# Linear attention gated by a Hadamard FFN on one core: spare VectorE work only where it fits, down's weights worked on 16 places behind their loads, layernorms queued in the output projection

## The chip, the cores and the metric

The kernel runs on one core of a Trainium2 chip. The metric is the device time in microseconds, as the median of several runs. The engines are named as in the profile: PE is TensorE (PEld its weight loads), DVE is VectorE, ACT is ScalarE, POOL is GpSimd, and SP is SyncE, which here does nothing but start DMA transfers, one after the other.

## The reference

`x` has 8 sequences of 512 tokens and 512 columns, all in float32. What is computed:

```python
xn  = layernorm(x)                                   # over the 512 columns
q, k, v = (xn @ W.T + b for W, b in ((Wq, bq), (Wk, bk), (Wv, bv)))
kv  = cumsum((elu(k) + 1) * v, axis=tokens)          # elementwise, along the sequence
s   = ((elu(q) + 1) * kv * 32**-0.5) @ Wo.T + bo
h   = fwht(xn * SU_ug) / 64                          # Walsh-Hadamard transform over 512 columns
up, gate = h @ W_up.T * scale_up, h @ W_gate.T * scale_gate      # 512 -> 2048
h   = fwht(silu(gate) * up * SU_dp) / 64             # over 2048 columns
g   = silu(h @ W_down.T * scale_dp)                  # 2048 -> 512
out = x + s * g
```

## The kernel before

**Tiling.** Two sequences make a pair, and the main loop runs over four pairs, p = 0 to 3. Every large product is a fast product: both operands are combined into seven factors (P1 to P7, each a sum or difference of quarters), seven half-size products are made, and VectorE adds them together while it reads them from PSUM. The weights' factors are made once, at p = 0, by VectorE and GpSimd, stored to DRAM (`keep_w`, `inner_w` with `d_gu`, `down_w` with `d_down`), and loaded from there in every later pair (`stream_w`). For `down`, whose weights also take the Hadamard transform, p = 0 first runs a chain over four blocks of 128 columns: load a block (`load_down`, L1062), scale it and run four butterfly levels on VectorE (`butterflies_down`, L1073 and L1078), let PE apply the remaining 128-point transform (`fold_down`, the four `pwd` matmuls of L1092), scale on ScalarE, store to `wd_f` (L1101). Then `first_half_down` loads it back by rows, encodes the factors and stores them in `d_down_0`, from which `w_down` is loaded.

**A pair.** `attention` makes k, v and q with cumsum and context; then four units u = 0 to 3 of the FFN follow: `gate` and `up` at p = 0, `hidden_unit` at p = 1 to 3 (it transforms with Hadamard levels on VectorE and GpSimd, whose result is `ho`). The output projection `project_out` (matmul L645, names `px_o`, `py_o`, `pz_o`) is interleaved with the end of unit 0. `down` runs after units 1 and 3. In between, tokens of the next pair are prepared: `normalized(b)` loads a sequence, takes its statistics (L201, L202), the root (L205), scales it (L210, L211) and stores it as `d_x`; `times_scales` multiplies by SU_ug on GpSimd and stores `d_xs`; `transforms` runs the Hadamard levels; `next_tokens` loads `z_x` and transposes it into the factors `xa`.

**Order.** The tile framework orders the instructions of each engine by priority, and each engine then executes its own list strictly in order; a wait at the head of it holds all that follows. Three devices set the order here:

- an agenda: `at(place, fn)` has a step issued `place` places later, where a place is two matmul instructions of 128x512 (0.86 us of PE) and `advance(n)` moves on;
- two lists of spare VectorE work: `later(us, fn, soon=)` queues a step with the time it is thought to take, in `urgent` (soon) or `idle`; `pace(ins, us)` issues from them behind a PSUM read `ins`, for about `us`; `catch_up()` issues all that is left at the end of a stage;
- `background()`, which lowers the priority by 150.

A weight is asked for by `ask(3)`, three entries ahead in a queue; `get_w` puts its encoding steps on the agenda. Buffers: six tiles in the pool `t8`, one in `xin`, four weights in `wpool`, PSUM banks px 3, py 1, pz 2, t 2.

The matmul lines are L569 (q, k, v, gate, up), L645 (o, down) and L747 (gate and up in `hidden_unit`). The PSUM reads of VectorE are L585 (at L569), L656 and L660 (at L645), L757 to L789 (at L747). ScalarE makes the snapshots `sa`, `sb`, `sc` of partial sums at p = 0 (L579, L581).

Two lines matter for what follows. In `inner_w` the fourth combination is written in the slot of the first, whose store must have landed:

```python
later(1.0, made, P5, 0, w1[:, 0], w1[:, 1], ALU.add, soon=True)
...
later(1.0, made, P7, 0, w0[:, 0], w1[:, 0], ALU.subtract, soon=True)
```

Of the kernel before, what the change touches and what calls it, by code (L numbers as in the profile page):

```python
# [21 lines left out]
def kernel(  # L22
# [67 lines left out]
    def pace(ins, us):  # L90
        while us > 0 and (urgent or idle):
            t, fn, args = (urgent or idle).pop(0)
            with tc.issue_after(ins.ins):
                fn(*args)
            us -= t
# [83 lines left out]
    def normalized(b, delay=12):  # L179


        if b > 3:
            t = xin.tile([P, 3, 7, P], F32, tag="x", name=f"x_{b}").rearrange("p c s e -> p (c s e)")
            xt = t[:, : NT * D].rearrange("p (n d) -> p n d", n=NT)
            su = t[:, NT * D : (NT + 1) * D]
        else:
            xt = t8.tile([P, NT, D], F32, tag="t", name=f"x_{b}")
        load_x(b, xt)
        if b > 3:
            nc.sync.dma_start(su, su_row.rearrange("o d -> (o d)").partition_broadcast(P))  # L190
        mv = small.tile([P, NT, 2], F32, tag="mv", name=f"mv_{b}")
# [28 lines left out]
        def times_scales():  # L220
            for t in range(NT):
                nc.gpsimd.tensor_tensor(xt[:, t], xt[:, t], su, ALU.mult)
            put("xs")
            if b % 2 == 0:
                at(8, lambda: normalized(b + 1, 10))

        def start():
            if b > 3:
                with background():
                    for t in range(NT):  # L230
                        stats(t)
                    root()
                    for t in range(NT):
                        scaled(t)
                    store()
                return
            for t in range(NT):
                later(0.8, stats, t)
            later(0.3, root)
            for t in range(NT):  # L240
                later(0.6, scaled, t)
            later(0.0, store)
# [45 lines left out]
    def next_tokens(b, xa):  # L288

        za, z = squares(f"x_{b}", xin), squares(f"x_{b + 1}", t8)  # L290
        turned(xa, P1, za, 0)
        turned(xa, P2, za, 1)

        def rest():
            turned(xa, P7, z, 0)
            turned(xa, P3, z, 1)
            outer_factors(xa)

        at(10, rest)

# [139 lines left out]
    def stream_w(name):  # L440
        w = new_w("%s_%s" % (name[0], name[1] if type(name[1]) is int else "%d_%d" % name[1]))
        if name[0] == "gu":
            u, i = name[1]
            nc.sync.dma_start(w, inner[u][:, i])
        elif name[0] == "down":
            h, i = name[1]
            while wd_made[h] < 4:
                assert urgent or idle
                _, fn, args = (urgent or idle).pop(0)
                fn(*args)  # L450
            w = by_factor(w, 4)
            nc.sync.dma_start(w, wd[h][:, i])
        else:
            nc.sync.dma_start(flat(w), kept["%s_%d" % name])
            if name[0] == "o":
                w = by_factor(w)
# [53 lines left out]
    def inner_w(m, u, w0, w1):  # L510
# [19 lines left out]
        later(1.0, made, P3, 2, w0[:, 1], t[:, 1], ALU.subtract, soon=True)  # L530
        later(1.0, made, P7, 0, w0[:, 0], w1[:, 0], ALU.subtract, soon=True)

# [268 lines left out]
    def attention(p, xo, co, get_w):  # L801
        def project(m, g, then):
# [4 lines left out]
            def whole(px):  # L807
# [4 lines left out]
                f"{m}_{p}_{g}", [w[:, 0], w[:, 1]], x_rhs(xo),  # L812
                (r[:, 0, 0], r[:, 1, 0], r[:, 1, 1]), whole, b, 1.7,
            )

        def elu_plus_one(r, name, then=None):
# [9 lines left out]
            half(0)  # L826
            at(5, lambda: half(1))

# [215 lines left out]
    def hidden_w(name, src, f):  # L1044
# [9 lines left out]

        return w, [(11, encode)]

# [5 lines left out]
    def load_down(o):  # L1062
        loaded.append(o)
        nc.sync.dma_start(rs[:, o % 2], wdown_t[:, o * P : (o + 1) * P].rearrange("(c p) e -> p c e", p=P))
# [48 lines left out]
    def first_w(m, g):  # L1113
# [4 lines left out]
        if m == "up":  # L1118
            return hidden_w(m, wup_t, g)
        name, eng = f"{m}_{g}", nc.gpsimd if m == "o" else nc.vector  # L1120
        if m == "o":
# [31 lines left out]
    def ask(n):  # L1153
        while queue and len(ahead) < n:
            p, m, g = queue.pop(0)
            w, steps = (first_w if p == 0 and m != "down" else later_w)(m, g)
# [68 lines left out]
    def begin_down():  # L1225
        nc.sync.dma_start(wsc_r, wscale_dp.partition_broadcast(P))
        load_down(0)
        at(12, lambda: chain_down(0))

    def chain_down(o):  # L1230
        if o not in loaded:
            at(4, lambda: chain_down(o))
            return

        def folded_block():
            fold_down(o)
            if o + 2 < KD:
                at(8, lambda: load_down(o + 2))
            if o + 1 == KD:
                at(8, first_half_down)  # L1240

        def then():
            at(14, folded_block)
            if o + 1 < KD:
# [5 lines left out]
        13: [lambda: normalized(2)], 14: [lambda: normalized(3)],  # L1250
        0: [lambda: first_transform(0, xa, xp, hads)], 1: [lambda: first_transform(1, xa, xp, hads)], 2: [begin_down],
        3: [lambda: load_down(1)], 4: [lambda: nc.sync.dma_start(bo_r, bo.partition_broadcast(P))],
    }
# [24 lines left out]
    for p in range(B // 2):  # L1278
# [12 lines left out]
        for u in range(NU):  # L1291
# [8 lines left out]
            else:  # L1300
                ho = new_h(f"ho_{p}_{u}")
                hidden_unit(p, u, xp, ho, get_w, u % 2 == 1)
                if u == 0 and more:
                    normalized(2 * p + 2)
                if u == 0:
# [67 lines left out]
```

## Time and profile before

| | |
|---|---|
| median of 3 runs | 1605.88 us (1604.14 to 1606.89) |
| the profiled execution | 1604.9 us |
| its span | 1603.1 us |
| granted TensorE clock, mean | 0.988 |
| PE busy | 1531.3 us (96%) |
| DVE, ACT, POOL busy | 1069.6, 394.8, 461.7 us |
| bytes moved by DMA | 285.74 MB, 178 GB/s over the span |

A row of the timeline has the start and the duration in microseconds from the start of the span, the engine, the line of the kernel, the operation, the tiles written and read by their names, the shape and the count; in brackets is how long the engine had been idle before, and what it was waiting for. A matmul in float32 counts twice in the profile, so four of 128x512 are two instructions of the kernel. A row of the groups has the busy time and the mean of one in nanoseconds, then the idle time before such rows with what ended most of it.

### The profile page before, as it was taken

The page shows a single profiled execution, that of the slowest core. Times are in us where ns is not written, and L with a number is a line of the kernel's source. Part 1 is how long each engine was busy: PE and PEld are TensorE (multiplying, and loading weights), DVE is VectorE, ACT ScalarE, POOL GpSimd, SP SyncE. Part 2 cuts the span into 40 slices and gives each one's busy share as a digit, 9 for nine tenths or more (in the row PEclk, how much of TensorE's full clock was granted, in tenths as well). Part 3 has the DMA queues.
Part 4 walks back from the last instruction along what each step waited for, and adds up shares of the span by engine and source line. Part 5 has one row for each costly group of instructions (what it writes and reads, how often), then busy time and mean ns, then how long its engine had stood idle before and what let it go on. Part 6 is the DMA issues. An engine that isn't in the chain of part 4 may idle for free. (4 is left out here: it accounts for less than half of the span.)

```text
span 1603.1 us, 15445 instructions
## 1 busy us (share of the span) xinstructions
PE 1531.3 (96%) x5808; PEld 1102.9 (69%) x5808; DVE 1069.6 (67%) x1444; ACT 394.8 (25%) x611; POOL 461.7 (29%) x262
## 2 busy tenths in 40 slices
PE   6987999999899999999999997999999999999998
PEld 3433636744674588788884486888887458888887
DVE  6896774465448984878664886688674686552673
ACT  4343321122014521112113431111211441111211
POOL 1034044012420363304510155300632116120731
PEclk9998999999999999999999999999999999999999
DMA  8327688776963357365677354736486524425462
GB/s 251 98 86 198 185 266 275 228 214 200 278 183 120 120 194 225 126 211 168 186 238 173 112 168 161 239 112 242 143 259 174 136 87 138 170 89 183 146 253 95
DMA packets 249034, 285.74 MB, mean 178 GB/s; under 512 B 98944, under 2 KB 200832, under 8 KB 244864
## 3 DMA queue, kind: packets, MB, share of 16 engines
q1 hardware_dynamic: 248288, 284.72, 57.7%
q8 instruction: 46, 0.75, 0.2%
q14 instruction: 28, 0.23, 0.0%
q10 hardware_dynamic: 672, 0.03, 0.0%
HBM read 200.31 MB, written 84.41 MB: 178 GB/s over the span
## 5 line engine op out<-in xcount | busy, mean ns | idle before, releaser
L645 PE MATMUL px_dn<-w_down,ho 128*128 128x256 f32 x1024 | 228.5, 379 | 0.0
L645 PEld LDWEIGHTS px_dn<-w_down,ho 128*128 128x128 f32 x1024 | 194.6, 190 | 28.2 <-issue 1.9
L747 PE MATMUL px_gu<-xi,w_gu 128*128 128x256 f32 x672 | 173.4, 380 | 2.8 <-DVE sa_gu L757 2.7
L747 PE MATMUL px_gu<-xp,w_gu 128*128 128x256 f32 x672 | 173.2, 379 | 1.3 <-DMA w_gu<-d_gu 1.3
L956 POOL TENSOR_TENSOR u<-u,v 128x1024 f32<-128x1024 f32 x24 | 56.1, 2360 | 347.6 <-DVE u L785 340.9
L747 PEld LDWEIGHTS px_gu<-xi,w_gu 128*128 128x128 f32 x672 | 126.7, 190 | 25.2 <-DVE sa_gu L757 3.9
L747 PEld LDWEIGHTS px_gu<-xp,w_gu 128*128 128x128 f32 x672 | 127.5, 190 | 20.6 <-DMA w_gu<-d_gu 2.1
L645 PE MATMUL pz_dn<-w_down,ho 128*128 128x256 f32 x496 | 112.9, 380 | 3.2 <-POOL ho L417 2.9
L645 PEld LDWEIGHTS pz_dn<-w_down,ho 128*128 128x128 f32 x496 | 93.5, 190 | 19.0 <-POOL ho L417 3.7
L747 PE MATMUL pz_gu<-xi,w_gu 128*128 128x256 f32 x336 | 87.8, 384 | 7.6 <-DVE u L778 6.4
L747 PE MATMUL pz_gu<-xp,w_gu 128*128 128x256 f32 x336 | 86.6, 380 | 2.0 <-DVE a L789 2.0
L414 POOL TENSOR_TENSOR co<-co 128x512 f32<-128x512 f32 x8 | 10.1, 1268 | 271.0 <-DVE co L850 271.0
L747 PE MATMUL py_gu<-xp,w_gu 128*128 128x256 f32 x336 | 86.3, 379 | 0.0
L1001 POOL TENSOR_TENSOR s<-s,d 128x512 f32<-128x512 f32 x30 | 39.0, 1299 | 159.0 <-ACT d L1000 119.9
L569 PE MATMUL px_gate<-xp,w_gate 128*128 128x512 f32 x128 | 63.3, 626 | 17.7 <-ACT sc_gate L579 10.1
L747 PEld LDWEIGHTS pz_gu<-xi,w_gu 128*128 128x128 f32 x336 | 63.8, 192 | 18.5 <-DVE u L778 8.0
L747 PEld LDWEIGHTS pz_gu<-xp,w_gu 128*128 128x128 f32 x336 | 63.5, 190 | 12.1 <-DVE a L789 3.6
L747 PEld LDWEIGHTS py_gu<-xp,w_gu 128*128 128x128 f32 x336 | 63.8, 190 | 9.1 <-DVE a L766 0.4
L960 POOL TENSOR_TENSOR v<-v,r 128x1024 f32<-128x1024 f32 x24 | 58.1, 2441 | 26.4 <-DVE r L785 17.9
L569 PE MATMUL px_v<-xa,w_v 128*128 128x512 f32 x128 | 62.4, 608 | 3.4 <-ACT sc_v L581 3.3
L645 PE MATMUL py_dn<-w_down,ho 128*128 128x256 f32 x256 | 60.7, 392 | 4.0 <-DMA w_down<-d_down 4.0
L569 PE MATMUL px_k<-xa,w_k 128*128 128x512 f32 x128 | 61.5, 603 | 2.0 <-ACT sc_k L581 1.6
(267 smaller groups left out, 2695.2 us busy)
## 6 DMA issues: line engine op xcount, KB each, us to landing
w_gu<-d_gu SPq DMA_DIRECT2D x84, 896.0 KB, 4.5
w_down<-d_down SPq DMA_DIRECT2D x56, 512.0 KB, 3.7
d_s<-o SPq DMA_DIRECT2D x8, 1024.0 KB, 5.6
d_d<-dn SPq DMA_DIRECT2D x8, 1024.0 KB, 6.5
d<-d_d SPq DMA_DIRECT2D x8, 1024.0 KB, 6.9
s<-d_s SPq DMA_DIRECT2D x8, 1024.0 KB, 8.1
y<-in_x_dram SPq DMA_DIRECT2D x8, 1024.0 KB, 8.3
out_dram<-y SPq DMA_DIRECT2D x15, 512.0 KB, 2.8
```

What stands on the lines that cost most here:

```text
L414: eng.tensor_tensor(o[..., P5, :], o[..., P7, :], o[..., P1, :], ALU.subtract)
L569: nc.tensor.matmul(p.rearrange("p a t -> p (a t)") if len(r.shape) == 2 else p, ws[k][:, i, :], r, start=(first and k == 0), stop=(k == n ...
L645: nc.tensor.matmul(p[:, c], t[:, (2 * g + c) * P : (2 * g + c + 1) * P], ws[i](k), start=(first and k == 0 and c == cs[0]), stop=(k == n - ...
L747: nc.tensor.matmul(p[:, lane], w[:, lane, i, :], x(i), start=(first and lane == 0), stop=True, skip_group_check=True,)
L956: nc.gpsimd.tensor_tensor(r[:, m], ru1[:, m], rv[:, m], ALU.add)
L960: nc.gpsimd.tensor_tensor(rv[:, m], rv[:, m], rr[:, m], ALU.add)
L1001: (nc.vector if final and (a, s) == (1, 0) else nc.gpsimd).tensor_tensor(r, r, d, ALU.mult)
```

## The change

- `pace` takes the head of a list only if that step's own time fits into what is left; before, it took one as long as anything was left. The time for an attention group is 2.4 instead of 1.7 us, and the second half of elu comes 7 places later instead of 5.
- Layernorms 4 to 7 are queued as spare work like 2 and 3, in place of being issued at lowered priority. `normalized(2p+2)` is called ahead of unit 0 with a delay of 47 places and `normalized(2p+3)` behind it with 10; before, the first was called behind unit 0 and the second from `times_scales` of the first. Odd sequences lie in a `t8` tile; the row SU_ug stays in the `xin` tile of the even one.
- `next_tokens` loads after 4 places, and queues its transposes 12 and 20 places after that; before, the loads came at once and the transposes at once and after 10.
- In `inner_w` the fourth combination is queued 8 places after the third.
- down's weights are not asked for until their four stores have been issued (`ask`); before, `stream_w` issued the queue until they were. A hidden weight's first encoding comes after 5 places (11). The encodings of w_o go to VectorE instead of GpSimd.
- Chain of down's blocks: it begins one plan step earlier; a block counts as loaded only 16 places after its load was started, and the chain asks every 2 places (4); the next load and `first_half_down` come after 6 places (8), the fold after 12 (14).

```diff
--- before.py
+++ after.py
@@ -88,7 +88,7 @@
         (urgent if soon else idle).append((us, fn, args))
 
     def pace(ins, us):
-        while us > 0 and (urgent or idle):
+        while (urgent or idle) and (urgent or idle)[0][0] <= us:
             t, fn, args = (urgent or idle).pop(0)
             with tc.issue_after(ins.ins):
                 fn(*args)
@@ -179,15 +179,15 @@
     def normalized(b, delay=12):
 
 
-        if b > 3:
+        if b > 3 and b % 2 == 0:
             t = xin.tile([P, 3, 7, P], F32, tag="x", name=f"x_{b}").rearrange("p c s e -> p (c s e)")
             xt = t[:, : NT * D].rearrange("p (n d) -> p n d", n=NT)
-            su = t[:, NT * D : (NT + 1) * D]
+            kept["su"] = t[:, NT * D : (NT + 1) * D]
         else:
             xt = t8.tile([P, NT, D], F32, tag="t", name=f"x_{b}")
         load_x(b, xt)
-        if b > 3:
-            nc.sync.dma_start(su, su_row.rearrange("o d -> (o d)").partition_broadcast(P))
+        if b > 3 and b % 2 == 0:
+            nc.sync.dma_start(kept["su"], su_row.rearrange("o d -> (o d)").partition_broadcast(P))
         mv = small.tile([P, NT, 2], F32, tag="mv", name=f"mv_{b}")
         rstd = small.tile([P, NT], F32, tag="rstd", name=f"rstd_{b}")
 
@@ -219,21 +219,10 @@
 
         def times_scales():
             for t in range(NT):
-                nc.gpsimd.tensor_tensor(xt[:, t], xt[:, t], su, ALU.mult)
+                nc.gpsimd.tensor_tensor(xt[:, t], xt[:, t], kept["su"], ALU.mult)
             put("xs")
-            if b % 2 == 0:
-                at(8, lambda: normalized(b + 1, 10))
 
         def start():
-            if b > 3:
-                with background():
-                    for t in range(NT):
-                        stats(t)
-                    root()
-                    for t in range(NT):
-                        scaled(t)
-                    store()
-                return
             for t in range(NT):
                 later(0.8, stats, t)
             later(0.3, root)
@@ -287,16 +276,23 @@
 
     def next_tokens(b, xa):
 
-        za, z = squares(f"x_{b}", xin), squares(f"x_{b + 1}", t8)
-        turned(xa, P1, za, 0)
-        turned(xa, P2, za, 1)
-
-        def rest():
-            turned(xa, P7, z, 0)
-            turned(xa, P3, z, 1)
-            outer_factors(xa)
-
-        at(10, rest)
+
+        def load():
+            za, z = squares(f"x_{b}", xin), squares(f"x_{b + 1}", t8)
+
+            def first():
+                turned(xa, P1, za, 0)
+                turned(xa, P2, za, 1)
+
+            def rest():
+                turned(xa, P7, z, 0)
+                turned(xa, P3, z, 1)
+                outer_factors(xa)
+
+            at(12, first)
+            at(20, rest)
+
+        at(4, load)
 
     def second_transform(xa, xp):
         t = xin.tile([P, 3, 7, P], F32, tag="x", name="z_again").rearrange("p c s e -> p (c s e)")
@@ -444,10 +440,7 @@
             nc.sync.dma_start(w, inner[u][:, i])
         elif name[0] == "down":
             h, i = name[1]
-            while wd_made[h] < 4:
-                assert urgent or idle
-                _, fn, args = (urgent or idle).pop(0)
-                fn(*args)
+            assert wd_made[h] == 4
             w = by_factor(w, 4)
             nc.sync.dma_start(w, wd[h][:, i])
         else:
@@ -528,7 +521,11 @@
         later(1.0, made, P5, 0, w1[:, 0], w1[:, 1], ALU.add, soon=True)
         later(1.0, made, P6, 1, t[:, 0], w0[:, 0], ALU.subtract, soon=True)
         later(1.0, made, P3, 2, w0[:, 1], t[:, 1], ALU.subtract, soon=True)
-        later(1.0, made, P7, 0, w0[:, 0], w1[:, 0], ALU.subtract, soon=True)
+
+        def last():
+            later(1.0, made, P7, 0, w0[:, 0], w1[:, 0], ALU.subtract, soon=True)
+
+        later(0.0, at, 8, last, soon=True)
 
 
 
@@ -810,7 +807,7 @@
 
             group(
                 f"{m}_{p}_{g}", [w[:, 0], w[:, 1]], x_rhs(xo),
-                (r[:, 0, 0], r[:, 1, 0], r[:, 1, 1]), whole, b, 1.7,
+                (r[:, 0, 0], r[:, 1, 0], r[:, 1, 1]), whole, b, 2.4,
             )
 
         def elu_plus_one(r, name, then=None):
@@ -824,7 +821,7 @@
                     then(h)
 
             half(0)
-            at(5, lambda: half(1))
+            at(7, lambda: half(1))
 
         def heads(g):
             phi = {}
@@ -1052,7 +1049,7 @@
                 with background():
                     inner_w(name, f - NU, encoded[name, f - NU], w)
 
-        return w, [(11, encode)]
+        return w, [(11 if encoded else 5, encode)]
 
     encoded = {}
     wd_f = dram.tile([FF, D], F32, tag="wd_f", name="wd_f")
@@ -1060,7 +1057,7 @@
     loaded = []
 
     def load_down(o):
-        loaded.append(o)
+        at(16, lambda: loaded.append(o))
         nc.sync.dma_start(rs[:, o % 2], wdown_t[:, o * P : (o + 1) * P].rearrange("(c p) e -> p c e", p=P))
 
     def butterflies_down(o, then):
@@ -1117,7 +1114,7 @@
             return hidden_w(m, wgate_t, g)
         if m == "up":
             return hidden_w(m, wup_t, g)
-        name, eng = f"{m}_{g}", nc.gpsimd if m == "o" else nc.vector
+        name, eng = f"{m}_{g}", nc.vector
         if m == "o":
             t = new_w(name)
             w = by_factor(t)
@@ -1152,7 +1149,15 @@
 
     def ask(n):
         while queue and len(ahead) < n:
-            p, m, g = queue.pop(0)
+            p, m, g = queue[0]
+            if m == "down" and wd_made[g[0]] < 4:
+                if ahead:
+                    break
+                while wd_made[g[0]] < 4:
+                    if not urgent and not idle:
+                        advance(1)
+                    catch_up()
+            queue.pop(0)
             w, steps = (first_w if p == 0 and m != "down" else later_w)(m, g)
             ahead.append({"key": (m, g), "w": w, "steps": steps, "traced": 0, "asked": 0, "place": 0})
 
@@ -1225,22 +1230,22 @@
     def begin_down():
         nc.sync.dma_start(wsc_r, wscale_dp.partition_broadcast(P))
         load_down(0)
-        at(12, lambda: chain_down(0))
+        chain_down(0)
 
     def chain_down(o):
         if o not in loaded:
-            at(4, lambda: chain_down(o))
+            at(2, lambda: chain_down(o))
             return
 
         def folded_block():
             fold_down(o)
             if o + 2 < KD:
-                at(8, lambda: load_down(o + 2))
+                at(6, lambda: load_down(o + 2))
             if o + 1 == KD:
-                at(8, first_half_down)
+                at(6, first_half_down)
 
         def then():
-            at(14, folded_block)
+            at(12, folded_block)
             if o + 1 < KD:
                 at(4, lambda: chain_down(o + 1))
 
@@ -1248,8 +1253,8 @@
 
     plan = {
         13: [lambda: normalized(2)], 14: [lambda: normalized(3)],
-        0: [lambda: first_transform(0, xa, xp, hads)], 1: [lambda: first_transform(1, xa, xp, hads)], 2: [begin_down],
-        3: [lambda: load_down(1)], 4: [lambda: nc.sync.dma_start(bo_r, bo.partition_broadcast(P))],
+        0: [lambda: first_transform(0, xa, xp, hads)], 1: [lambda: first_transform(1, xa, xp, hads), begin_down],
+        2: [lambda: load_down(1)], 4: [lambda: nc.sync.dma_start(bo_r, bo.partition_broadcast(P))],
     }
     for n, u, j in ((16, 2, 0), (17, 2, 1), (18, 3, 0), (19, 3, 1)):
         plan.setdefault(n, []).append(lambda u=u, j=j, n=n: down_w(u, j, rd[:, (n - 16) % 3 * 1792 : (n - 16) % 3 * 1792 + 1792]))
@@ -1299,9 +1304,11 @@
                     up(p, u + m * NU, gs[m], xp, ho[:, m], get_w)
             else:
                 ho = new_h(f"ho_{p}_{u}")
+                if u == 0 and more:
+                    normalized(2 * p + 2, 47)
                 hidden_unit(p, u, xp, ho, get_w, u % 2 == 1)
                 if u == 0 and more:
-                    normalized(2 * p + 2)
+                    normalized(2 * p + 3, 10)
                 if u == 0:
                     project_out(p, co, get_w)
             hos.append(ho)
```

## The prediction

> **What bounds the kernel now.** I read the page's busy shares first, then the groups for what ended PE's waits, then PE's timeline around each wait, then the VectorE (DVE) timeline at the same places.
>
> ```profile
> span 1603.1 us, 15445 instructions
> PE 1531.3 (96%) x5808; PEld 1102.9 (69%) x5808; DVE 1069.6 (67%) x1444; ACT 394.8 (25%) x611; POOL 461.7 (29%) x262
> ```
> PE is the bound: 71.8 us of the span is not PE. Nothing in this change alters the matmuls, so only PE's waits, and the slow matmuls after them, can move the time. Undisturbed starts lie 1.72 us apart for four 128x512 (or eight 128x256), shown with 1.88 or 1.89 busy.
>
> ```profile
> 108.93 3.75 PE L569 MATMUL px_gate<-xp,w_gate 128*128 128x512 f32 x4 [4.67 <-DVE w_gate L423]
> 112.48 3.14 PE L569 MATMUL pz_q<-xa,w_q 128*128 128x512 f32 x4
> 151.51 3.78 PE L569 MATMUL px_gate<-xp,w_gate 128*128 128x512 f32 x4 [10.12 <-ACT sc_gate L579]
> 430.38 6.40 PE L645 MATMUL py_dn<-w_down,ho 128*128 128x256 f32 x16 [3.96 <-DMA w_down<-d_down]
> 968.11 2.08 PE L747 MATMUL pz_gu<-xi,w_gu 128*128 128x256 f32 x4 [5.47 <-DVE u L778]
> 983.65 1.99 PE L645 MATMUL pz_o<-w_o,co 128*128 128x256 f32 x8 [3.56 <-DVE u L789]
> ```
> These five waits, the number in brackets, are the large ones that the change touches. The row after each is slow: 3.75 and 3.14 for 1.88 are 1.9 and 1.3 lost again.
>
> ```profile
> 140.88 1.09 DVE L525 TENSOR_TENSOR s_gate<-w_gate,w_gate 128x896 f32<-128x896 f32 x1 [10.46 <-DMA d_gu<-s_gate]
> 146.84 2.36 DVE L1078 TENSOR_TENSOR xi<-xi 128x1024 f32<-128x1024 f32 x2 [4.87 <-DMA xi<-in_wdown_t_dram]
> 149.12 0.68 DVE L585 TENSOR_TENSOR g<-sb_gate,pz_gate 128x512 f32<-128x512 f32 x1
> 966.78 0.69 DVE L201 BATCH_NORM_STATS2 st<-x 128x6 f32<-128x512 f32 x1 [6.86 <-DMA x<-in_x_dram]
> 977.54 4.86 DVE L211 TENSOR_SCALAR x<-x,mv,rstd 128x512 f32<-128x512 f32 x3
> ```
> So PE's 10.12 is not ScalarE's: VectorE stood for a slot whose store had not landed, then for down's block 2, with the PSUM read `g<-sb_gate` queued behind. At 966 it stood for x_7's load, at 977 it worked on x_7, each time ahead of a read.
>
> ```profile
> 60.00:100.00 40.00, 39.89 (x94) 17.53 (x93) 40.00 (x42) 16.72 (x21) 8.27 (x5) 1.00 0.32 99
> 100.00:110.00 10.00, 5.33 (x12) 2.10 (x11) 10.00 (x13) 3.61 (x4) 5.86 (x4) 0.91 0.23 92
> 110.00:130.00 20.00, 20.00 (x42) 8.59 (x41) 20.00 (x24) 15.10 (x41) 10.37 (x2) 0.88 0.26 74
> ```
> Windows (busy PE, PEld, DVE, ACT, POOL, then clock, DMA share, GB/s): from 60 to 130 us VectorE has no idle time at all. What leaves one place there turns up at another.
>
> **The change part by part.** All durations are from the one profiled execution (1604.9; span 1603.1 and 1.8 around it; the median of the runs shown is 1.0 higher). Places in the queues come from laying the two kernels' instruction orders side by side.
>
> 1. *The 4.67 wait.* The encodes of w_gate now come right behind down's block 0, at about 99, so this wait goes with its 1.9 + 1.3 of slow matmuls: 7.9. But PE's four matmuls `pwd` (L1092) of block 1 keep their place, and need block 1's last butterfly. Summing VectorE's rows in the new order, with the eight w_o encodes (8 x 0.41 = 3.3) moved there from GpSimd, it ends at about 121.4; PE, no longer held, gets there at about 114.8. New wait 6.6 plus some 2 of slow matmuls. Net 0. The bounds: −3 (if the encodes collide with GpSimd) to +7.9 (if the wait does not form).
> 2. *The 10.12 wait.* P7 is put 8 places later, and block 2 is worked on 16 places after its load. P5 is made at about 125, its store takes 4.8 to land, P7 comes at about 135; block 2 lands at about 125 and is used at about 136. So neither wait is left, and `g<-sb_gate` isn't held: 10.12 + (3.78 − 1.88) + (2.33 − 1.89) = 12.5, of which I take 12.0 because the reads ahead still have to drain.
> 3. *Down's first half.* `pwd` of block 3 moves some 35 us later, behind the gate of unit 1, and w_down's first load is now asked for only after all four d_down stores. In the new order the last four encodes of `wd` follow the read of u_0_1: 0.68 + 4 x 0.34 to 0.78 (w_gate's encodes from start to start; wd's own mean) + store 0.5 + 5.1 + load 0.5 + 3.7 = 11.8 to 13.6, while PE has four groups of 1.72 = 6.9 left. New wait 5 to 6.7, with 2 to 3 of slow matmuls, less the 1.7 wait of 272 us that goes: −6.7. Before, that load was issued 14 us early (243.19, used at 257.64): this cover is gone.
>
> ```profile
> L94 DVE TENSOR_TENSOR wd<-wd 128x256 f32<-128x256 f32 x8 | 6.1, 784 | 0.1
> d_down<-wd SPq DMA_DIRECT2D x2, 896.0 KB, 5.1
> w_down<-d_down SPq DMA_DIRECT2D x56, 512.0 KB, 3.7
> 243.19 1.89 SPq L452 DMA_DIRECT2D w_down<-d_down  x2
> ```
> The mean of one encode (784 ns), the time from issue to landing of the store (5.1) and of the load (3.7), and when the load was issued. On SP, stores of s_up now stand ahead of this load; they are ready earlier than d_down, so they add nothing.
> 4. *w_down of the second half.* It now goes to SP ahead of the z_x loads (next_tokens waits 4 places). The 3.96 wait goes with 2.8 of slow matmuls: +6.8. The transposes are queued at 12 and 20 places instead of at once and 10; they still end before the attention that reads them: 0 (ends: 0, and −2.7 where the last four, 0.68 each, drain ahead of it).
> 5. *Losses of 3.4 at 207 and 227* (stores and loads that SP held): a third of them go, +1.
> 6. *Layernorms 4 to 7.* Those of p=2 held PE 5.47 + 1.9 at 968 and 3.56 + 0.1 at 983: 11.1. Now their steps are queued behind the 14 reads of the output projection, 14 x 1.73 = 24.2 us of PE. By rows, reads 14 x 0.65 = 9.1; one layernorm is 4 x 0.72 (statistics, 0.60 + 0.12 from start to start) + 1.9 (root 1.78, reciprocal 0.16) + 4 scalings. L211 takes 0.48 alone (1.92 for four) and 1.62 when GpSimd works on `ho` beside it (4.86 for three); 0.885 is its mean in the groups. Two layernorms: 13.4 to 22.5, 16.7 at the mean. 9.1 + 16.7 = 25.8 against 24.2: 1.6 too much, and with 0.5 for the slower matmuls behind a held read I charge 2.1 (ends: 0 and 7.4). Net +9.0. In p=1 waits of 2.25 (533 us) and some 1.5 (561 to 584) go, and the same charge comes: +1.5.
> 7. *SP.* Two more loads of x and a store stand ahead of w_gu_1_6 in each o stage: −0.8 (ends 0 and −3). x_7's tile in t8 is used again by u3; its store lands some 17 us after the stage, u3 starts at 21.7: covered, by 5 us.
> 8. *Attention's group time 2.4 and elu's 7 places* move the same set of steps; the small waits of 866, 891 and 911 stay: 0. Freed GpSimd time is worth nothing, since it isn't waited for there.
>
> Sum: 0 + 12.0 − 6.7 + 6.8 + 1.0 + 9.0 + 1.5 − 0.8 = 22.8. 1604.9 − 22.8 = 1582.1; plus 1.0 for the median: 1583.
>
> **Two rules weighed.** Slow matmuls: the rows show 10.12 followed by +2.3, 4.67 by +3.1, 3.96 by +2.8, but 3.56 by only 0.1. The Trainium skill, "TensorE: Matmul & The Clock Gate" (Part 1: The HAM clock gate), has the clock halve after an idle window of about 3.4 us. A window at a free phase fits these rows; it means that cutting a long wait into pieces under 3 us gains 2 to 3 us even at equal idle. For part 6 it makes the charge of 2.1 complete; for the wait of part 3 it adds the 2 to 3. Taking the rows of waits alone, the sum would be about 5 lower.
> Collision: 1.62 for 0.48. "SBUF — State Buffer" (Who interferes with whom) says that VectorE in its two-port mode and GpSimd lock each other out for a whole instruction. This speaks against part 6: GpSimd's `ho` rows are 2.36 each, and with every scaling locked out for one, the two layernorms would be 9.6 + 8 x (0.48 + 2.36) = 32.3, with the reads 41.4 against 24.2, a charge of 17.2 for 2.1. With it in both p = 1 and p = 2 the sum would be 22.8 − 2 x 15.1 = −7.4, about 1613: slower. The trace had 1.62 for one even in its worst place, where GpSimd worked without a pause (three rows of `ho` in 7.26); so I stay with the rows.
>
> **The rivals.**
> - *VectorE is full and the waits only move.* For it: the windows, and parts 1 and 6 that don't fit. Then part 2 gives 8 (the reads behind it are late), part 6 gives 2 instead of 10.5: 22.8 − 12.5 = 10, about 1595. Chance 0.22.
> - *No new waits at pwd or w_down.* Part 1 pays 7.9 and part 3 costs 0: 22.8 + 7.9 + 6.7 = 37, about 1568. Against it: VectorE's rows summed. 0.10.
> - *Slower: down's weights come late.* Asking for w_down now first empties VectorE's queue. If much of unit 1's encoding is still in it (four matrices, some 7.5 us each), up to 30 us go before the store. It decides from a wait of about 32 at dn_0_0, 26 more than in part 3; with the queue full it is 6 + 30, and the sum 22.8 − 30 = −7: about 1613. Against it: in the new order only the last steps of s_up follow. 0.13.
> - *Nothing measurable,* the parts cancelling: 0.07. That the change does not do what it says is excluded by the orders.
> The main case has 0.48.
>
> **The numbers.** 0.2%, 3.2 us, is about what a measurement of this kernel tells from no change. Faster: 0.48 + 0.22 + 0.10 = 0.80; same 0.07; slower 0.13. The range runs from 1565 (no new waits) to 1606 (takes in the bounds of 1, 6 and 7 together, but not the slower case).
>
> **What would show it.** Right: no wait at px_gate<-sc_gate of over 3 us; a wait of PE at pwd on DVE xi near 115; one at px_dn on DMA w_down near 250 of 5 to 7; none at py_dn near 415; waits under 3 us in the o stages at 560 and 950, with L211 there. Wrong: a px_dn wait over 15, L211 near 2.4 in the o stages, u3 (L956) waiting for the store of xs_7, or px_gate still waiting for a store of s_gate.

## The result: slower by 0.28%

| | before | after |
|---|---|---|
| median | 1605.4 us (8 runs) | 1609.95 us (8 runs) |
| ratio, 95% interval | 1 | 1.0028 (1.0017 to 1.0039) |
| profiled execution (span) | 1604.9 (1603.1) | 1610.57 (1608.8) |

The forecast of 1583, with a range of 1565 to 1606, had the wrong sign. The page of the changed kernel:

```profile
span 1608.8 us, 15435 instructions
PE 1536.9 (96%) x5808; PEld 1106.3 (69%) x5808; DVE 1085.5 (67%) x1452; ACT 391.3 (24%) x608; POOL 456.4 (28%) x254
```
The span is 5.7 longer, and PE's busy time 5.6: the rows behind waits are slower, and the total waiting is the same 71.9. A sum hides what happened, so the two traces have to be laid beside each other. PE does the same matmuls in both. I added up their counts times their undisturbed distance (0.4292 us for 128x512, 0.2158 for 128x256), and compared the times at which the two kernels had done equal amounts (in a stretch without waits, for example, the same `pz_q` starts at 69.38 before and at 62.77 after). The difference of these times changes in steps; minus is time won:

| PE's time before | change | what stands there |
|---|---|---|
| to 69 | −6.6 | wait ph<-DVE xh of 4.5 gone |
| 69 to 190 | −8.0 | waits 4.67 and 10.12 gone; new ones of 2.2, 2.9, 3.0 |
| 190 to 243 | +7.0 | pwd of block 3: waits 1.8 and 6.0 |
| 243 to 294 | +16.7 | w_down of the first half: waits 0.7, 3.2, 8.1, 1.8 |
| 294 to 454 | −7.2 | wait py_dn<-w_down of 3.96 gone |
| 454 to 608 | −2.7 | layernorms of p = 1 |
| 608 to 633 | +6.8 | w_gu waited for |
| 633 to 939 | +1.0 | attention of p = 2, less small gains |
| 939 to 1000 | −10.9 | layernorms of p = 2 |
| 1000 to 1026 | +7.7 | w_gu waited for |
| 1026 to 1306 | +1.6 | attention of p = 3 |
| to the end | 0.0 | |

That is 35.4 won and 40.9 lost (5.5 at the last matmul, 5.7 over the span). PE's timeline after the change: the first row is the wait at pwd that part 1 foresaw, the others carry the losses.

```profile
114.86 3.63 PE L1089 MATMUL pwd<-xi,had 128*128 128x512 f32 x4 [2.93 <-DVE xi L1070]
...
215.74 3.78 PE L1089 MATMUL pwd<-xi,had 128*128 128x512 f32 x4 [6.00 <-ACT xi L1095]
...
256.18 1.99 PE L566 MATMUL pz_up<-xp,w_up 128*128 128x512 f32 x4 [3.20 <-DVE u L582]
266.24 8.27 PE L642 MATMUL px_dn<-w_down,ho 128*128 128x256 f32 x24 [8.08 <-DMA w_down<-d_down]
...
633.06 1.36 PE L744 MATMUL px_gu<-xp,w_gu 128*128 128x256 f32 x4 [4.61 <-DMA w_gu<-d_gu]
...
1013.43 2.08 PE L744 MATMUL px_gu<-xp,w_gu 128*128 128x256 f32 x4 [5.25 <-DMA w_gu<-d_gu]
```
All five waits of before are gone or small. In their place stand two chains that got late (215 to 266) and two loads that PE had not waited for (633, 1013). The lines of the kernel are some three lower than before the change: L1092 is now L1089, L645 is L642, L747 is L744.

**Why w_down is late.** VectorE's timeline at the end of the chain, in front of the 3.20 and the 8.08:

```profile
202.34 4.49 DVE L1070 TENSOR_TENSOR xi<-r 128x1024 f32<-128x1024 f32 x2
...
249.24 0.67 DVE L582 TENSOR_TENSOR u<-sb_up,pz_up 128x512 f32<-128x512 f32 x1
249.83 5.70 DVE L94 TENSOR_TENSOR wd<-wd 128x256 f32<-128x256 f32 x4
255.45 0.67 DVE L582 TENSOR_TENSOR u<-sc_up,pz_up 128x512 f32<-128x512 f32 x1
```
GpSimd's timeline beside it:

```profile
250.05 2.40 POOL L915 TENSOR_TENSOR ho<-g,u 128x1024 f32<-128x1024 f32 x1 [1.69 <-DVE u L582]
252.53 1.32 POOL L411 TENSOR_TENSOR ho<-ho 128x512 f32<-128x512 f32 x1
253.81 1.44 POOL L413 TENSOR_TENSOR ho<-ho 128x512 f32<-128x512 f32 x1
```
The last four encodes took 5.70, where the same form had taken 1.55 for four ten microseconds earlier. One by one they took 0.41, 2.45, 1.48 and 1.48: the first was over soon after GpSimd began, and each of the others ended 0.3 us behind one of GpSimd's three operations. They hold the read of `sc_up`, which is PE's 3.20. The last store to d_down is issued at 255.56, the load at 260.04, PE goes on at 266.24. The chain is late from the butterflies on: the eight of block 3 now run between 181 and 207, in pairs of up to 4.49 (one alone up to 3.36, against 1.21), again beside GpSimd's `ho`. Before, they had run between 171 and 183 at 2.35 a pair, with GpSimd idle until 186:

```profile
180.76 2.35 DVE L1073 TENSOR_TENSOR xi<-r 128x1024 f32<-128x1024 f32 x2
```

**Why w_gu is late.** SP's queue after the output projection of p = 2:

```profile
1000.16 0.37 SPq L197 DMA_DIRECT2D d_xs<-x  x1
1001.95 0.37 SPq L197 DMA_DIRECT2D d_x<-x  x1
1002.38 1.03 SPq L865 DMA_DIRECT2D d_s<-o  x1
1003.52 2.41 SPq L440 DMA_DIRECT2D w_gu<-d_gu  x2
```
The loads of w_gu stand behind d_xs of sequence 6 (GpSimd's scaling), d_x of sequence 7 (VectorE's last L211 ends at 1001.9), and d_s. Before, only d_s was close ahead, and w_gu was issued at 1003.21:

```profile
1002.36 0.81 SPq L868 DMA_DIRECT2D d_s<-o  x2
1003.21 8.32 SPq L444 DMA_DIRECT2D w_gu<-d_gu  x3
```
```profile
1012.56 1.13 PE L747 MATMUL px_gu<-xp,w_gu 128*128 128x256 f32 x4 [0.51 <-DMA w_gu<-d_gu]
```
PE, 4 us earlier than before by then, needed the load at 1008 and got it at 1013.4, 0.9 later than before: what the layernorms had gained was waited for here. At p = 1 the load itself got late. It was issued at 623.74 (before: 619.68) and landed 9.3 later (before: 6.7); PE came to it only 0.8 earlier. Both times the DMA engines were busy from the load's issue to its landing (a mean share of 1.02 and 1.03), so the 1 MB stores just ahead of it count twice: for when it is issued, and for how long it takes.

### The profile page after: what moved, and what is told of

It reads as the page before. It is cut to its first block, busy times and chain, and to the rows that moved or that the text cites. A ratio compares the mean times of both kernels' runs of the same rounds, so it can differ in the third digit from the quotient of the medians.

```text
span 1608.8 us, 15435 instructions
## 1 busy us (share of the span) xinstructions
PE 1536.9 (96%) x5808; PEld 1106.3 (69%) x5808; DVE 1085.5 (67%) x1452; ACT 391.3 (24%) x608; POOL 456.4 (28%) x254
## 4 chain that ended last, share of the span: by engine, by line
PE 76%; DVE 14%; DMA 3%; issue 2%; ACT 2%; POOL 1%; SPq 1%; POOLq 0%; DVEq 0%; ACTq 0%
PE px_gu L744 16%; PE px_dn L642 13%; PE pz_gu L744 8%; PE pz_dn L642 5%; PE py_gu L744 4%; PE py_dn L642 4%; PE px_o L642 3%; PE px_k L566 3%; PE px_q L566 2%; PE px_up L566 2%; PE px_v L566 2%; PE px_gate L566 2%; PE pz_o L642 2%; DVE xp L94 1%; PE pz_v L566 1%
## 5 line engine op out<-in xcount | busy, mean ns | idle before, releaser
L642 PE MATMUL px_dn<-w_down,ho 128*128 128x256 f32 x1024 | 231.0, 382 | 8.8 <-DMA w_down<-d_down 8.1
L642 PEld LDWEIGHTS px_dn<-w_down,ho 128*128 128x128 f32 x1024 | 196.4, 192 | 38.0 <-issue 9.8
L744 PE MATMUL px_gu<-xp,w_gu 128*128 128x256 f32 x672 | 174.3, 382 | 10.8 <-DMA w_gu<-d_gu 9.9
L744 PE MATMUL px_gu<-xi,w_gu 128*128 128x256 f32 x672 | 173.3, 380 | 0.0
L744 PEld LDWEIGHTS px_gu<-xp,w_gu 128*128 128x128 f32 x672 | 127.7, 191 | 31.6 <-DMA w_gu<-d_gu 10.7
L744 PEld LDWEIGHTS px_gu<-xi,w_gu 128*128 128x128 f32 x672 | 127.6, 191 | 21.2 <-issue 2.2
L642 PE MATMUL pz_dn<-w_down,ho 128*128 128x256 f32 x496 | 112.3, 379 | 1.3 <-POOL ho L413 1.3
L642 PEld LDWEIGHTS pz_dn<-w_down,ho 128*128 128x128 f32 x496 | 93.7, 190 | 15.6 <-POOL ho L413 1.7
L744 PE MATMUL pz_gu<-xp,w_gu 128*128 128x256 f32 x336 | 88.4, 385 | 0.5 <-DVE a L786 0.5
L744 PE MATMUL py_gu<-xp,w_gu 128*128 128x256 f32 x336 | 88.1, 385 | 0.0
L744 PE MATMUL pz_gu<-xi,w_gu 128*128 128x256 f32 x336 | 86.6, 380 | 1.3 <-DVE u L775 1.2
L744 PEld LDWEIGHTS pz_gu<-xp,w_gu 128*128 128x128 f32 x336 | 64.7, 193 | 10.8 <-DVE a L786 1.7
L744 PEld LDWEIGHTS pz_gu<-xi,w_gu 128*128 128x128 f32 x336 | 63.5, 190 | 11.4 <-DVE u L775 2.9
L744 PEld LDWEIGHTS py_gu<-xp,w_gu 128*128 128x128 f32 x336 | 64.8, 193 | 9.4 <-DVE a L763 0.3
L913 POOL TENSOR_TENSOR ho<-g,u 128x512 f32<-128x512 f32 x8 | 13.6, 1702 | 177.7 <-DVE u L582 177.7
```

Source lines behind the costliest of these rows:

```text
L642: nc.tensor.matmul(p[:, c], t[:, (2 * g + c) * P : (2 * g + c + 1) * P], ws[i](k), start=(first and k == 0 and c == cs[0]), stop=(k == n - ...
L744: nc.tensor.matmul(p[:, lane], w[:, lane, i, :], x(i), start=(first and lane == 0), stop=True, skip_group_check=True,)
L913: nc.gpsimd.tensor_tensor(ho[:, P1], g[:, 0, 0], r[:, 0, 0], ALU.mult)
```

## The experiments

Each ratio is of the run to the kernel before, with its 95% interval; the changed kernel has 1.0028. Differences between profiles are those of PE's times at equal work, as above. They tell where time is won or lost; how much, they tell less well. The changed kernel was not run again beside these runs, and the kernel before took 1593.5 to 1608.9 there; the profiles of the first three runs below end 5.7 to 6.0 ahead of the changed kernel's, which their ratios don't show.

**Stores of the layernorms on GpSimd's queue**

```diff
-            nc.sync.dma_start(d.rearrange("(n p) d -> p n d", p=P), xt)
+            (nc.gpsimd if b > 3 else nc.sync).dma_start(d.rearrange("(n p) d -> p n d", p=P), xt)
```


> The changed kernel, with only the stores of d_x and d_xs of layernorms 4 to 7 moved from SP's queue to GpSimd's. Theory (order on SP): in the changed kernel the loads of w_gu stand on SP behind d_xs, d_x and d_s, which wait for VectorE's layernorm (w_gu issued at 623.74 and 1003.52, used 9.3 and 9.9 us later; PE waits 4.61 and 5.25, with slow matmuls 6.8 and 7.3). With those stores elsewhere both waits shrink to under 1: 12 to 14 us less than the changed kernel, about 1597. Rival (bandwidth): the loads are slow because 1 MB stores run beside them, whoever issues them; then at most 3 us less, 1607 or more.

1.0031 (1.0012 to 1.0050): nothing won in the time. In its profile the waits at 633 and 1013 are gone: the first w_gu load is issued at 616.47, not 623.74, lands in 5.9, not 9.3, and 6.3 and, at p = 2, 8.5 are won at these places. But 7.4 and 7.3 are lost again behind them, at 651 and 1029:

```profile
650.83 2.07 PE L744 MATMUL px_gu<-xp,w_gu 128*128 128x256 f32 x4 [5.55 <-DMA w_gu<-d_gu]
```
```profile
641.03 0.57 SPq L265 DMA_DIRECT2D z_x<-d_x  x1
641.69 2.73 SPq L440 DMA_DIRECT2D w_gu<-d_gu  x2
```
On SP a load z_x now waits 10.2 for GpSimd's `x` (L222), with w_gu behind it; GpSimd itself had waited 13.1 for its own store d_x to land. So neither theory holds as written. The order on SP made the wait, and moving two stores away only let the next waiting entry of the queue do the same.

**pace as before**

```diff
-        while (urgent or idle) and (urgent or idle)[0][0] <= us:
+        while us > 0 and (urgent or idle):
```


> The changed kernel, with pace as before (a step is taken as long as any time is left). Theory (down's chain is late because pace now takes less per read): block 3's butterflies, spread over 181 to 207 us in the changed kernel, are issued closer together; pwd of block 3 stands some 9 groups (15 us) earlier; the waits for ACT xi at 216 (6.0) and for w_down at 266 (8.1, and 3.2 of VectorE ahead of it) go almost all: 12 to 20 us less, 1590 to 1598; some of it is lost again by reads that stand behind overfilled VectorE. Rival (it is asking for w_down only after all stores): the wait for w_down stays over 6, and the time at 1607 or more.

1.0026 (1.0010 to 1.0043). The mechanism came as expected, the 12 to 20 us in the time did not: there is no wait for w_down at p = 0, and the profile is 23.4 ahead of the changed kernel by 250 us, in spite of 6.8 lost by 130 us (waits of 3.34 and 6.22 for VectorE). Most of it is lost again later: waits for w_gu of 8.43 and 8.53 (5.5 and 4.2 more around the two places), for w_down of 5.42 and 5.67 at p = 2 and 3 (7.1 and 8.2). So the new pace costs p = 0 and saves the later pairs.

**Attention's time at 1.7**

```diff
-                (r[:, 0, 0], r[:, 1, 0], r[:, 1, 1]), whole, b, 2.4,
+                (r[:, 0, 0], r[:, 1, 0], r[:, 1, 1]), whole, b, 1.7,
```


> The changed kernel, with an attention group's time back at 1.7 us. Theory: the waits pz_v<-DVE v of 2.12 near 920 and 1301 us, with slow matmuls around them (2.2 and 3.4 more lost than before the change), come from two steps queued behind one read; they go back to 1.7 and less: 3 to 5 us less at p = 2 and 3; at p = 0 the chain of down gets less time per read and later by a few us: net -3 to +3. Rival: those waits come from elu's 7 places: then they stay, and only the loss at p = 0 shows, +2 to +6.

1.0021 (1.0005 to 1.0037). In the profile it is about as the theory had it: 2.7 and 2.8 less at p = 2 and 3, and at p = 0 a lead of 10 by 230 us that ends as a wait for w_down of 19.6.

**Blocks 2 and 3 first in the queue**

```diff
-            later(1.2, scale, i)
+            later(1.2, scale, i, soon=o > 1)
...
-                later(1.2, half, i, dst, src, h)
+                later(1.2, half, i, dst, src, h, soon=o > 1)
-        later(0.0, then)
+        later(0.0, then, soon=o > 1)
```


> The changed kernel, with the scaling and butterflies of down's blocks 2 and 3 queued as soon (in urgent, ahead of the rest). Theory (block 3's chain is late): pwd of block 3 stands 5 groups (8.6 us) earlier, the wait for w_down at 266 (8.08 and 2.9 slow) shrinks to under 3 and the wait for ACT xi at 216 (6.0) to under 2: 10 to 16 us less than the changed kernel, 1594 to 1600. Rival (asking late is the cause, whenever the chain ends): 3 us less at most. Second rival (VectorE is full there): the wait moves to a gate or up read between 160 and 250, and nothing is gained.

0.9945 (0.9925 to 0.9964): faster than both kernels. The profile leads the changed one by 18.2 at 257 us, and keeps it (18.1 at the end; by the ratios it is 13). PE's rows there, and at w_gu, which this edit leaves alone:

```profile
247.36 8.07 PE L642 MATMUL px_dn<-w_down,ho 128*128 128x256 f32 x24 [4.57 <-DMA w_down<-d_down]
...
615.96 2.07 PE L744 MATMUL px_gu<-xp,w_gu 128*128 128x256 f32 x4 [4.61 <-DMA w_gu<-d_gu]
```
pwd of block 3 comes at 195.9 instead of 206.9 and waits for nothing. The wait for w_down is 4.57, more than the "under 3" expected, but the 3.20 and the 6.00 are gone. Both rivals fall: asking late is the same here, and no other read took the wait over.

**The layernorms as before, on top of that.** `normalized` and its calls are those of the kernel before the change.

> The kernel of e10_soon (0.9945 of before), with the layernorms of sequences 4 to 7 placed and issued as before the change. It measures what the layernorm part is worth. Theory (order on SP): the waits for w_gu (4.61 and 4.65 with slow matmuls, 13 us together) go, and the waits of before at 533 to 584 and 961 to 984 (3.7 and 11.1) come back: within 4 us of e10_soon, a ratio of 0.993 to 0.998. Rival (bandwidth): the waits for w_gu have nothing to do with the layernorms' stores ahead of them, stay, and the old ones come on top: a ratio of 1.003 or more.

0.9970 (0.9948 to 0.9991), inside the band of the theory. The waits for w_gu are small (0.56 and 1.12), and from there on 8.9 and 6.6 are won; the waits of before are back (5.46 at 564, 3.48 at 948), and 11.4 and 10.8 are lost around them. So the layernorm part, which gains 13.6 in its own stages, is worth only some 4 (by the ratios) to 7 us (in the profile).

**The odd layernorm 40 places after unit 0**

```diff
-                    normalized(2 * p + 3, 10)
+                    normalized(2 * p + 3, 40)
```


> The kernel of e10_soon, with the odd layernorm of each pair (5 and 7) started 40 places after unit 0 instead of 10, so that on SP its stores come behind five loads of w_gu instead of ahead of them. Theory (order on SP): PE's waits for w_gu at about 616 and 997 shrink from 4.6 to under 1.5 each, with their slow matmuls: 8 to 13 us less than e10_soon, a ratio of 0.986 to 0.990. Rival (bandwidth: the d_s stores and the loads share the engines): at most 3 us less. Second rival (the later layernorm now holds reads of unit 1): the waits go, and others of the same size come between 620 and 700: 0.993 to 0.997.

1.0048 (1.0026 to 1.0069): slower by some 16 us than the kernel it starts from. The waits for w_gu fell to 1.90 and 2.41, worth 5.4 and 3.9; that side of the theory held in part. The second rival was right, and larger than it said: 13.1 and 12.7 are lost behind them. VectorE and then PE at 698 to 704:

```profile
698.50 2.36 DVE L246 TENSOR_TENSOR xh<-xs 128x1024 f32<-128x1024 f32 x2 [4.93 <-DMA xs<-d_xs]
...
703.17 0.68 DVE L657 TENSOR_TENSOR dn<-sb_dn,pz_dn 128x512 f32<-128x512 f32 x1
```
```profile
703.91 0.70 PE L744 MATMUL pz_gu<-xp,w_gu 128*128 128x256 f32 x2 [2.32 <-DVE dn L657]
```
The Hadamard levels of that sequence wait for its late d_xs, VectorE stands with the read of `dn` behind, and the levels then pile up ahead of unit 2's reads.

**The same with attention at 1.7.** The edits of e10_soon, f2_soon_odd40 and e4_time17 together.

> The kernel of f2_soon_odd40, with an attention group's time back at 1.7 us. Theory: in the run with 1.7 alone the waits for v went (2.8 less at p = 2, 3.6 at p = 3) and 3.5 were won between 119 and 149 us, while the wait for w_down at p = 0 grew to 19.6; with down's blocks 2 and 3 ahead in the queue the latter does not come: 5 to 9 us less than f2_soon_odd40. Rival (blocks 0 and 1, worked on in attention, set the chain's end): w_down's wait is 8 or more, and it is as slow as f2_soon_odd40 or slower.

1.0183 (1.0130 to 1.0236). The rival was right: blocks 0 and 1 are worked on during attention, and with less time there the chain ends late whatever is done for blocks 2 and 3. The wait for w_down is 20.8, with 9.6 of VectorE ahead of it.

**P7 at once again**

```diff
-        def last():
-            later(1.0, made, P7, 0, w0[:, 0], w1[:, 0], ALU.subtract, soon=True)
-
-        later(0.0, at, 8, last, soon=True)
+        later(1.0, made, P7, 0, w0[:, 0], w1[:, 0], ALU.subtract, soon=True)
```


> The kernel of e10_soon, with the fourth combination of inner_w (P7) queued at once again. Theory (part 2 of the prediction): VectorE again waits for the slot's store, up to 10 us at the first unit (the wait of px_gate<-ACT sc_gate near 150) and a few at the others: 6 to 14 us more than e10_soon, a ratio of 0.998 to 1.003. Rival (the new placing of block 2 alone took the wait away, P7 comes late enough anyhow): within 2 us of e10_soon.

0.9937 (0.9914 to 0.9960), not told apart from e10_soon. No wait of 10 us comes back near 150. The 8 places for P7, one of the two causes that part 2 of the prediction named for its gain, are worth nothing measurable here. They move waits: without them the 3.59 at 144 of e10_soon is gone (4.3 won), and the wait for w_down is 8.31 instead of 4.57.

**Attention at 1.7 for p = 1 to 3 only**

```diff
-                (r[:, 0, 0], r[:, 1, 0], r[:, 1, 1]), whole, b, 2.4,
+                (r[:, 0, 0], r[:, 1, 0], r[:, 1, 1]), whole, b, 1.7 if p else 2.4,
```


> The kernel of e10_soon, with an attention group's time at 1.7 us for p = 1 to 3 and at 2.4 for p = 0 only. Theory: the two waits pz_v<-DVE v of 2.12 (and the slow matmuls near them) go, 2.8 at p = 2 and 3.6 at p = 3 as in e4_time17, and p = 0 stays as in e10_soon: 4 to 7 us less than e10_soon, a ratio of 0.990 to 0.992. Rival (with less taken behind each read, work is left for the end of the attention, where it holds the first hidden unit): within 2 us of e10_soon.

0.9914 (0.9887 to 0.9942); the waits for v at p = 2 and 3 are gone (2.8 each in the profile). The intervals of this run and e10_soon overlap.

**And d_x of the odd layernorm 12 places later**

```diff
-            later(0.0, store)
+            later(0.0, (lambda: at(12, store)) if b > 3 and b % 2 else store)
```


> The kernel of g1_soon_t17p, with the store d_x of layernorms 5 and 7 (and what follows it) put 12 places later; VectorE's work stays where it is. On SP this lets two w_gu loads go ahead of d_x, and d_xs come after four. Theory (order on SP makes PE wait for w_gu): the waits of 4.6 near 614 and 995 shrink to 2.5 or less, 4 to 5 us each with the slow matmuls: 7 to 11 us less than g1, a ratio of 0.984 to 0.987. Rival (the loads land late because d_s and the stores share the DMA engines): at most 3 us less. Second rival (as in f2_soon_odd40, what follows d_xs gets late and holds unit 2): no gain or a loss.

0.9879 (0.9845 to 0.9913): the fastest of all, 1584.5 us against 1605.7 for the kernel before beside it, and 5.6 less than g1_soon_t17p, where 7 to 11 were expected. Its PE row at the place of the 4.61:

```profile
617.15 1.13 PE L744 MATMUL px_gu<-xp,w_gu 128*128 128x256 f32 x4 [1.92 <-DMA w_gu<-d_gu]
```
At 991 it is 2.06. The profile is 7.2 ahead of g1's: 4.3 and 5.3 at the two loads, and 2.8 of it lost again elsewhere. VectorE's work is where it was; only the place of two stores on SP differs. This is what e1_store_pool had not shown: a change of the order on SP alone takes more than half of the wait. The traces also tell how. At equal work of PE the load is issued 1.6 us earlier than in g1's and lands in 8.2 instead of 9.3, which together are the 2.7 by which the wait of p = 1 shrinks. The remaining 1.9 is time to land: half of all w_gu loads of the changed kernel land within 4.5, but here d_s is still under way, and the DMA engines are busy from issue to landing (share 1.02 again). So the rival, that stores slow the loads, has a part in it.

**The kernel before, with the 16 places and the new asking alone**

```diff
-        loaded.append(o)
+        at(16, lambda: loaded.append(o))
...
-            at(4, lambda: chain_down(o))
+            at(2, lambda: chain_down(o))
             return
```
(and `ask` as in the change, since w_down would otherwise be asked for before its stores)

> The kernel before, with two parts of the change alone: a block of down counts as loaded only 16 places after its load was started (asked every 2 places), and down's weights are not asked for until their stores have been issued. Theory (each wait that this removes early comes back at w_down): the wait for DVE xh of 4.46 at 39 us goes (6 us with slow matmuls), the 10.12 at 151 shrinks by the 4.87 of block 2's load or more; block 3 ends later than before even with pace as before, and a wait for w_down of 5 to 15 comes at about 255: within 8 us of before, a ratio of 0.996 to 1.005. Rival (the late chain is pace's doing alone): no wait for w_down over 2, and 10 to 16 us less than before, a ratio of 0.990 to 0.994.

1.0120 (1.0080 to 1.0160), worse than either theory had it. It leads before by 13.5 at 175 us: the waits for `xh` and for block 2 are gone (a wait of 4.51 at 141 stands in place of the 10.12), so the 16 places are what won there. Then 25.9 are lost from 250 to 300:

```profile
259.97 3.78 PE L566 MATMUL pz_up<-xp,w_up 128*128 128x512 f32 x4 [6.87 <-DVE u L582]
...
278.76 6.42 PE L642 MATMUL px_dn<-w_down,ho 128*128 128x256 f32 x16 [15.02 <-DMA w_down<-d_down]
```
With pace as before, pwd of block 3 comes at 224 instead of 187, and w_down is waited for longer than in the changed kernel. So the late chain is not pace's doing alone. Each block may start no earlier than 16 places after its load, and its load not until the block two before it is folded.

**The kernel before, with the new asking alone.** Only `ask` and `stream_w` are changed.

> The kernel before, with one part of the change alone: down's weights are not asked for until their four stores have been issued. Theory (the lateness of the chain makes the wait for w_down, not the way of asking): the stores are issued at about 227 us, w_down is needed at 258; within 3 us of before, a ratio of 0.998 to 1.002. Rival (asking late is the cause): a wait for w_down of over 5 near 258, a ratio of 1.003 or more.

1.0007 (0.9988 to 1.0026), no difference: asking late costs nothing where the stores are early. It also leaves the wait py_dn<-w_down (3.57) as it was, so that gain of the change is not from the asking. That it is from the later z_x loads, as part 4 had it, was not tried alone.

## Why the prediction was wrong

- *Part 1* (net 0): 0.1 lost. The wait at pwd of block 1 was 2.9 instead of 6.6, and one of 2.2 stands ahead of it. *Part 2* (12.0): 7.7. At the place of the 10.12 it was 12.6, as in the sum, but 4.9 was lost just behind it, against the 0.5 that was taken off: PE waits 2.98 at 144 for another read `g`, and VectorE had stood 2.83 for a load of w_up ahead of it. The reason was half wrong: in e5_before_16 the wait shrinks without P7's delay, and in f4_soon_last0 it doesn't come back.
- *Left out of the list:* the wait ph<-DVE xh, 6.4 with its slow matmuls:

```profile
34.45 2.36 DVE L1078 TENSOR_TENSOR xi<-xi 128x1024 f32<-128x1024 f32 x2 [5.40 <-DMA xi<-in_wdown_t_dram]
```
```profile
39.26 1.48 PE L378 MATMUL ph<-xa,xi 128*128 128x512 f32 x2 [4.46 <-DVE xh L386]
```
VectorE stood there for block 0's load, as at 146 for block 2's, and the same 16 places removed it (e5_before_16 too). I had looked at this row in the groups and taken it as not touched. How long this wait is differs between executions: in e9_before_ask, which does nothing to it, it is 1.78.
- *Part 3 is the step that failed first.* It set new waits of 5 to 6.7 and 2 to 3 of slow matmuls against the 1.7 that goes: 6.7. From 243 to 294 it cost 16.7. The term that was mis-sized most is the last four encodes: 1.4 to 3.1 in the sum, 5.70 on the chip, which hit twice, as the read behind them (3.20) and in the chain (17.0 from the read of u to w_down in use, against 11.8 to 13.6). The load then took 6.2 from issue to use, against 4.2; the store was 1.1 faster. The size of the encodes stood in the trace of before, where three of them had run beside GpSimd; the mean of 784 ns hid it:

```profile
221.43 4.29 DVE L94 TENSOR_TENSOR wd<-wd 128x256 f32<-128x256 f32 x3
```
The other 7.0, the wait of pwd of block 3 for ScalarE, had no term at all. I had seen that it moves 35 us later, and priced only what follows it. ScalarE's silu ahead of it waited for a read that stood behind VectorE's butterflies and encodings. e10_soon, which changes nothing but when blocks 2 and 3 are worked on, takes 16.5 of these 23.7 back in its profile (13 of the time, by the ratios).
- *Part 4* (+6.8): 7.2. Right in size; that the later z_x loads did it was not tried alone.
- *Part 5* (+1) can't be told apart from the rest of its stretch.
- *Part 6* (+9.0 and +1.5): 10.9 and 2.7. Right, and the charge of 2.1 was too much. Of the eight L211 in the o stage of p = 1 six took 0.53 to 0.55 us and two 1.00 and 1.49, beside GpSimd's scalings of L222; at p = 2 it is the same. GpSimd had no `ho` there. So the rule of the Trainium skill, "SBUF — State Buffer" (Who interferes with whom), by which the sum would have been −7, did not decide here, and that the time came out near that sum is chance. But I had set the rule aside for a wrong reason: the 1.62 "even in its worst place" is a mean of 1.92, 2.56 and 0.53, and the first two each ended 0.3 behind an `ho` row of GpSimd. And tensor_tensor work with both inputs in SBUF, which that section also has contending with GpSimd's reads, was slowed at the other place: 1.2 to 3.4 for a butterfly, 0.4 to 2.45 for an encode. I had weighed the rule on the wrong part.
- *Part 7* (−0.8, ends 0 and −3) failed too: −14.6. I counted the entries on SP and not what they wait for, nor that PE already came to this load as it landed. d_x of the odd sequence can't be issued before VectorE's last scaling, and w_gu stands behind it: that made the load late at p = 1. At p = 2 the load was hardly later, and PE came 4 us earlier to it because of the gain of part 6.
- *Part 8* (0) was wrong by some 5: the waits for v cost 2.5 more than before at p = 2 and as much at p = 3, and e4_time17 takes 2.7 and 2.8 back.
- *The rivals.* "Slower: down's weights come late" has the right place and not its mechanism: VectorE's queue was not emptied ahead of the store, the chain was late as a whole. It got 0.13, because its price was set so that it had to outweigh all gains by itself. Together with w_gu half of that price was enough. "VectorE is full and the waits only move" was half right on 190 to 294 us: waits moved there, and VectorE had no idle time from 177 to 215, but from 215 to 260 it was busy for only 21.7 of 45 us.
- *The clock.* Waits of 6.00 and 8.08 are followed by 2.6 and 2.9 of slow matmuls, 5.25 by 3.1 and 4.61 by 1.8; the granted clock was 0.58 from 215 to 222 us and 0.70 from 266 to 276. Part 3 had counted 2 to 3 for it. Its other inference, that pieces under 3 us gain, does not hold: the waits of 2.93 and 2.98 are followed by 1.8 each.

## What to carry to other kernels

When a change removes waits at one place, ask for every transfer on an in-order DMA queue what the entries ahead of it wait for, not only how many there are: a load that was just in time becomes the bound as soon as the compute ahead of it gets faster. A chain of work that is moved later has to be priced beside its new neighbours (here GpSimd's operations, beside which an encode took 1.5 to 2.5 us instead of 0.41), and each link of it, not only the last. A mean over rows with and without such a neighbour gives the price of neither. If spare work feeds a chain with a deadline, put it ahead of the spare work that has none: here one flag on two blocks turned a loss of 0.28% into a gain of 0.55%.

## What the runs showed of the hardware that was not expected

- The same encode of 128x256 on VectorE took 0.39 each at 239 us (1.55 for four), with GpSimd idle. At 250 us it took as long as GpSimd's operation beside it: 2.45 beside one of 2.40, 1.48 beside 1.32 and 1.44. VectorE's reads of PSUM among them kept their 0.67 (249.24 and 255.45).
- The 1 MB store d_x of sequence 5 landed in 5.3 us where it was issued ahead of the w_gu loads (the changed kernel), and in 11.7 and 13.8 with loads under way beside it: in g2_store12 on SP's queue, in e1_store_pool on GpSimd's.
